# A stack of four graph layers on one core: four batches in one sequence, score rows by way of DRAM, a pace for each stage

## The chip, the cores and the metric

The kernel runs on one core of a Trainium2 chip. The metric is the time of one execution in device microseconds (us). The kernel before was timed three times: 3205.61 us is the median, 3198.1 and 3207.4 the ends. A further execution was taken by the hardware profiler.

The engines by the names of the profile: PE is TensorE (PEld its weight loads), DVE VectorE, ACT ScalarE, POOL GpSimd, SP SyncE, which here only issues transfers. Each engine works through its own queue in order. Work on one waits for another through semaphores.

## The reference

Sixteen batches of 1024 nodes with 256 features (`x`), and one adjacency matrix `adj` (1024 x 1024, a few entries in each row). Four layers, one after the other, all in float32:

```python
# layer 0, h = x: an edge score for each pair of nodes
hidden = relu(h @ W1[:d] per u  +  h @ W1[d:] per v  +  b1)
S   = sigmoid(hidden @ W2 + b2)
a   = einsum('buv,bud->bvd', S * adj, h)
m   = einsum('uv,bud->bvd', adj, h) * h
z   = beta1*h + beta2*(a @ Wa + ba) + beta3*(m @ Wm + bm)
# layer 1
z   = z + relu(einsum('ij,bjd->bid', adj, z) @ W.T + b)
# layers 2 and 3, each with its own weights
f   = z @ W1.T
f1  = f @ W2 + b2
c   = softmax(leaky_relu(f1[:, :, None] + f1[:, None, :]) + adj)
z   = c @ f + bias2 + z
```

Scores are needed only where `adj` is not zero.

## The kernel before

**Groups.** The sixteen batches are four groups of four (`GB`). The time falls into a first stage, and then one pass for each group, which has an edge stage and the layers 1 to 3.

**The scores.** `score_steps` is a generator that computes the edge scores of all groups, one step for one neighbour (a "slot") of 128 nodes in four batches at once. There are 616 steps: 8 that find the neighbours, then 152 for each group. A step is: an indirect gather of 128 rows into a tile `z` by POOL (L695; issued four steps ahead, six tiles), an addition and a product on VectorE (L805, L807), four sums along rows on ScalarE (L811). After the last slot of a tile the sigmoid follows and the results `gt` are put on the list `waiting`, from which indirect scatters write them into a dense matrix `dense_d` in DRAM (L700), one or two behind each gather. At the last tile of a group (L830 to L834) all that still waits is scattered at once, and the group is put on `finished`.

**Pace.** The class `Side` runs these steps along a main stage. Main stages are generators too; each `yield` tells some us of TensorE work, and the steps that are owed are these us times a rate: `RATE[0]`, 0.26, in the first stage and `RATE[1]`, 0.255, in all others. As each engine's instructions stand in the order that this makes (a scheduler of the framework then moves some a little ahead or back by what it holds to be ready), the rate sets how much score work stands between two instructions of a main stage. A group may be used only when its scores are `finished`; where the pace was too low, the missing steps are run with no main stage beside them.

**First stage** (to about 961 us): products that need no scores, for all sixteen batches, with the scores of group 0 and part of those of group 1.

**Edge stage** (`with_edges`): for four column blocks and eight row tiles, `gd` is loaded from `dense_d` by SP (L886), reordered by ScalarE into `gc` (L1064), and multiplied with `hw` into eight banks of PSUM; it waits for all scatters of the group.

**Layers** (`pair_layers`): of a group's four batches two go through layers 1 to 3 and then the other two. For a pair: layer 1 (`projected`, `neighbours`, with `adjT_in` read by SP, L1124), then for layers 2 and 3 and each batch a `front` (features `f` for all nodes, with the node's score as column 257) and two halves of `sums`. In `sums`, VectorE makes a tile `m` from the row `r` of all scores, `ta`, and exp(adj) (L1036, four buffers), TensorE multiplies it with `f` into four banks; then the result is scaled and turned back. `scales` stands between `front` and `sums`: it brings the column of 1024 scores to a row on all partitions by nine 128 x 128 transposes of a broadcast column (L1002, and L1007 for the maximum), and takes the exponentials.

`scales` and `turn_back` are put on the list `later` and are run in the middle of the next stage, by `catch_up` at the second tile of a front or the first of a half. After the fronts of the second pair `ahead` loads `hw` and `z` of the next group (L892, L900), all eight at once on SP.

**Last group.** There are no scores left to compute then. While its first pair goes through the layers, the neighbours' sums of the second pair for six of eight node tiles are computed from lists by gathers and VectorE (`by_lists`, L1172 to L1176, with the first product of a list on ScalarE, L1174), paced by `far_ahead`: 0.88 steps a us for the first 68 us, then 0.58.

Of the kernel before, what the change touches and what calls it, by code (L numbers as in the profile page):

```python
# [19 lines left out]
RATE = (0.26, 0.255)  # L20
# [45 lines left out]
def gnn_stack_kernel(  # L66
# [120 lines left out]
    class Attention:  # L187


        def __init__(self, W1, W2, b2, bias2, name):  # L190
# [5 lines left out]
            self.rows = const.tile([P, DH, P], F32, name=f"{name}_rows")  # L196

        def prepare(self, nat):
# [8 lines left out]
            nc.vector.tensor_copy(self.wT[:, :, D], ps[:, :DH])  # L207
            for dh in range(DH):
                nc.vector.tensor_copy(self.rows[:, dh, :], self.wT[:, dh, D : D + 1].to_broadcast([P, P]))
# [26 lines left out]
    def prepare(t):  # L236
        transpose_weight(l1wT, t[:, 0])
        for i, gat in enumerate((gat2, gat3)):
            gat.prepare(t[:, 1 + i])
# [22 lines left out]
    part_d = dram.tile([XT * P + P, 2 * D], F32, name="part_d")  # L262

# [411 lines left out]
    with tc.If(listed > 0) as arm:  # L675
        with ExitStack() as stack:
# [27 lines left out]
            def score_steps(pool):  # L704
# [75 lines left out]

                moved, got, arrive = None, None, 0
                later = mybir.DependencyClass.NoSync
                for n, (g, t, k) in enumerate(todo):
                    if n + LEAD < len(todo):
                        last = fetch(us, zt, *todo[n + LEAD])
                    for _ in range(0 if n < HOLD else 2 if n % 2 and len(waiting) > 4 else 1):
                        if waiting:
# [3 lines left out]
                            after(tc, ins, [last], later, "behind the gather")  # L791
                    if moving:
# [25 lines left out]
                    if k == slots - 1:  # L818
# [11 lines left out]
                        if t == last_of[g]:  # L830
                            for group, *what in waiting:
                                group.add(scatter(*what))
                            waiting.clear()
                            finished.append(g)  # L834
# [25 lines left out]

            class Side:
# [5 lines left out]
                def along(self, main, rate=1):  # L867
                    for us in main:
                        self.owed += us * rate
# [37 lines left out]
            with ExitStack() as first:  # L907
# [48 lines left out]
                side.along(with_zeros(score_free()), RATE[0])  # L956
# [12 lines left out]
            def front(x, weights):  # L969
# [3 lines left out]
                for jt in range(NT):  # L973
# [7 lines left out]
                    if jt == 1:  # L981
                        catch_up()
                    yield 0.86
                made = {}
                later.append(lambda: scales(f, weights, made))
                return made

            def scales(f, weights, made):
# [4 lines left out]
                ta = small.tile([P, NT], F32, tag="tau", name="tau")  # L993
# [16 lines left out]
                for v in range(NV):  # L1010
                    nc.scalar.activation(r[:, v * HN : (v + 1) * HN], banks[v], AF.Relu, bias=sh[:, 3:4])
                nc.vector.tensor_scalar(sh[:, 1:2], sh[:, 0:1], -0.01, None, ALU.mult)
# [8 lines left out]
            later = []  # L1021

            def catch_up():
                while later:
                    later.pop(0)()

            def sums(made, v, finish):

                if "f" not in made:
                    catch_up()  # L1030
# [3 lines left out]
                for jt in range(NT):  # L1034
# [9 lines left out]
                    if jt == 0:  # L1044
                        catch_up()
# [73 lines left out]
            def neighbours(y, z, cols):  # L1119
                n = cols.stop - cols.start  # L1120
                acc = [[bank() for _ in range(DH)] for _ in range(2)]
                for jt in range(NT):
                    a = three.tile([P, HN], F32, tag="a", name="adjT_in")[:, :n]
                    nc.sync.dma_start(a, adjT_d[jt][:, cols])  # L1124
                    for i in range(2):
                        for eh in range(DH):
# [3 lines left out]
                            )  # L1130
# [315 lines left out]
```

## Time and profile before

| | |
|---|---|
| median of three executions | 3205.61 us |
| the profiled execution, its own time | 3224.95 us |
| its span (first to last instruction) | 3223.1 us |
| granted TensorE clock, mean | 0.990 |
| TensorE busy | 3127.4 us |
| VectorE, ScalarE, POOL busy | 2349.9, 1955.7, 1819.4 us |
| bytes moved | 687.48 MB |

Some groups of the profile, by line:

| line, engine, what | count | busy us | mean ns |
|---|---|---|---|
| L126 PE, products with `m` | 4096 | 923.3 | 383 |
| L126 PE, products with `gc` | 2048 | 456.6 | 384 |
| L1002 PE, transposes in `scales` | 256 | 35.4 | 274 |
| L805 DVE, score, addition | 608 | 738.9 | 1220 |
| L807 DVE, score, product | 608 | 738.0 | 1220 |
| L1036 DVE, `m` | 512 | 375.6 | 744 |
| L811 ACT, score, sums | 2432 | 979.8 | 407 |
| L1064 ACT, `gc` | 128 | 265.2 | 2074 |
| L695 POOL, gathers for scores | 512 | 645.9 | 1261 |
| L700 POOL, scatters | 512 | 642.5 | 1255 |

A float32 product is two instructions in the profile (4096 for 2048 products of the sums), a transpose is one. Matmuls are pipelined, so the mean of one is longer than what it adds: 64 instructions of the sums follow one another in 13.88 us. The edge stages begin at about 961, 1540, 2116 and 2687 us of the span, and the layers follow each.

### The profile page before, as it was taken

To read this page: it belongs to the slowest core of one execution; us is meant where nothing else is said; L and a number is where in the kernel's file an instruction comes from. 1 tells how busy PE (TensorE), PEld (TensorE's weight loads), DVE (VectorE), ACT (ScalarE), POOL (GpSimd) and SP (SyncE) were. 2 spreads that over 40 slices of the span, in tenths; PEclk is the share of its full clock that TensorE was granted. 3 is DMA by queue.
4 is the path that set the end of the run, shared out by engine and by line. 5 is a ranking of instruction groups with operands and counts; after the bars stand their busy time and mean duration, and the time that the engine had idled before them with its cause. 6 is when DMAs were issued, how large, how long until landed. Compare 5 with 4: busy or idle time off the path is not lost. (4 is left out here: it accounts for less than half of the span.)

```text
span 3223.1 us, 39246 instructions
## 1 busy us (share of the span) xinstructions
PE 3127.4 (97%) x12122; PEld 2203.7 (68%) x12122; DVE 2349.9 (73%) x3162; ACT 1955.7 (61%) x6524; POOL 1819.4 (56%) x1483
## 2 busy tenths in 40 slices
PE   8899999999999999999999999899999999998999
PEld 5444544545557668678876867777587688857888
DVE  7797767677774789789768978877798891147744
ACT  3245555666668767567977756688676774413342
POOL 1146778676764656657666665556676652076500
PEclk9999999999999999999999999999999999999999
DMA  9899898888889755756876575587657644485600
GB/s 315 292 323 322 267 288 263 265 242 249 271 284 343 211 167 150 229 158 203 300 233 171 158 212 177 161 284 239 187 151 212 181 145 145 131 256 154 156 7 28
DMA packets 281994, 687.48 MB, mean 213 GB/s; under 512 B 45280, under 2 KB 137440, under 8 KB 274608
## 3 DMA queue, kind: packets, MB, share of 16 engines
q0 software_dynamic: 128224, 387.80, 41.6%
q1 hardware_dynamic: 126112, 245.98, 22.2%
q10 hardware_dynamic: 27440, 51.13, 4.2%
q8 instruction: 97, 1.59, 0.2%
q14 instruction: 121, 0.99, 0.1%
HBM read 553.45 MB, written 131.32 MB: 212 GB/s over the span
## 5 line engine op out<-in xcount | busy, mean ns | idle before, releaser
L811 ACT ACTIVATE z<-z 128x256 f32<-128x256 f32 x2432 | 979.8, 407 | 642.3 <-DVE z L807 568.8
L805 DVE TENSOR_TENSOR z<-z,u 128x1024 f32<-128x1024 f32 x608 | 738.9, 1220 | 435.9 <-PE bank L126 291.9
L126 PE MATMUL bank<-feats,m 128*128 128x257 f32 x4096 | 923.3, 383 | 19.0 <-DVE m L1036 17.8
L695 POOL DMA_INDIRECT z<-v_d,slot_v x512 | 645.9, 1261 | 477.1 <-ACT z L811 264.1
L126 PEld LDWEIGHTS bank<-feats,m 128*128 128x128 f32 x4096 | 771.4, 191 | 138.4 <-DVE m L1036 19.8
L700 POOL DMA_INDIRECT dense_d<-gt,slot_at x512 | 642.5, 1255 | 186.8 <-issue 139.5
L807 DVE SCALAR_TENSOR_TENSOR z<-z,w2r 128x1024 f32<-128x1024 f32 x608 | 738.0, 1220 | 9.0
L126 PE MATMUL bank<-gc,hw 128*128 128x256 f32 x2048 | 456.6, 384 | 25.0 <-ACT gc L1064 17.8
L811 ACT ACTIVATION_READ_ACCUMULATOR z<-z 128x1 f32 x2432 | 463.3, 190 | 0.0
L126 PEld LDWEIGHTS bank<-gc,hw 128*128 128x128 f32 x2048 | 388.6, 192 | 92.5 <-ACT gc L1064 25.9
L126 PE MATMUL bank<-adj_sb,h 128*128 128x512 f32 x1024 | 443.0, 592 | 4.0 <-ACT st L322 2.4
L1036 DVE SCALAR_TENSOR_TENSOR m<-rho,tau,adj_sb 128x512 f32<-128x512 f32 x512 | 375.6, 744 | 72.1 <-PE bank L126 68.5
L126 PE MATMUL bank<-adjT_in,y 128*128 128x512 f32 (+1 forms) x960 | 401.2, 578 | 3.9 <-DMA adjT_in<-adjT_d 2.5
L126 PEld LDWEIGHTS bank<-adj_sb,h 128*128 128x128 f32 x1024 | 194.3, 190 | 244.2 <-issue 239.6
L126 PE MATMUL bank<-w,hT 128*128 128x512 f32 (+1 forms) x1024 | 336.2, 489 | 0.0
L126 PEld LDWEIGHTS bank<-adjT_in,y 128*128 128x128 f32 x960 | 181.9, 190 | 218.9 <-issue 204.3
L1064 ACT ACTIVATE gc<-gd 128x1024 f32<-128x1024 f32 x128 | 265.2, 2074 | 94.0 <-PE bank L126 59.1
L126 PEld LDWEIGHTS bank<-w,hT 128*128 128x128 f32 x1024 | 195.7, 192 | 143.0 <-issue 121.0
L126 PE MATMUL bank<-g_wT,z 128*128 128x257 f32 x1024 | 233.7, 383 | 8.2 <-DVE z L1117 8.2
L695 POOL DMA_INDIRECT z<-v_d,x_node x96 | 123.4, 1285 | 176.7 <-ACT z L811 115.7
L126 PEld LDWEIGHTS bank<-g_wT,z 128*128 128x128 f32 x1024 | 193.2, 191 | 39.0 <-DVE z L1117 8.9
L322 ACT ACTIVATE st<-bank 128x512 f32<-128x512 f32 x128 | 75.6, 590 | 104.3 <-PE bank L126 62.5
(161 smaller groups left out, 2403.2 us busy)
## 6 DMA issues: line engine op xcount, KB each, us to landing
gd<-dense_d SPq DMA_DIRECT2D x128, 512.0 KB
dense_d<-zero ACTq DMA_DIRECT2D x64, 512.0 KB
adjT_in<-adjT_d SPq DMA_DIRECT2D x112, 256.0 KB
h<-in_x_dram SPq DMA_DIRECT2D x19, 1024.0 KB
u_d<-st SPq DMA_DIRECT2D x64, 256.0 KB
v_d<-st SPq DMA_DIRECT2D x64, 256.0 KB
hw_d<-st SPq DMA_DIRECT2D x64, 256.0 KB
u<-u_d POOLq DMA_DIRECT2D x32, 512.0 KB
```

The source lines that it names most:

```text
L126: recent.append(nc.tensor.matmul(*args, **kw))
L322: nc.scalar.activation(st[:, c, :2, :], ps.rearrange("p (s k) -> p s k", s=2), AF.Copy)
L695: return nc.gpsimd.indirect_dma_start(out=dst, out_offset=None, in_=src[:], in_offset=bass.IndirectOffsetOnAxis(ap=at, axis=0), **how,)
L700: return nc.gpsimd.indirect_dma_start(out=dst[:], out_offset=bass.IndirectOffsetOnAxis(ap=at, axis=0), in_=src, in_offset=None,)
L805: paced(nc.vector.tensor_tensor(z, z, u, ALU.add))
L807: nc.vector.scalar_tensor_tensor(zk, zk, 0.0, w2r[:, None, :].to_broadcast([P, GB, D]), ALU.max, ALU.mult)
L811: nc.scalar.activation(zk[:, c, :], zk[:, c, :], AF.Copy, accum_out=s[:, k, c : c + 1])
L1036: nc.vector.scalar_tensor_tensor(m, r[:, cols], ta[:, jt : jt + 1], ea[:, jt, cols], ALU.max, ALU.mult)
L1064: paced(nc.scalar.activation(gc, gd.rearrange("p n i -> p i n"), AF.Copy), 16)
```

## The change

- **Order.** `group_layers` takes the four batches of groups 0 to 2 as one sequence: layer 1 for the first two, the first front, layer 1 for the other two, and then for the eight pairs of layer and batch the next one's front ahead of this one's two halves of sums. `hw` and `z` of the next group are loaded one after the other during the last two of these eight. The last group keeps `pair_layers`.
- **Rows through DRAM.** In `group_layers`, `scales` is replaced by `to_row` (the column and its maximum by one transpose to 9 rows, stored to `row_d`, and read back as a broadcast to all partitions, all on SP) and `from_row`, three ticks later. A tick is every second tile of a half, every fourth of a front, every tile of `neighbours`. The tiles `rows` are then needed only in the other branch of the program, which does not run.
- **Pace.** The rate is chosen by stage: 0.295 in edges and layer 1, 0.26 in fronts, 0.212 in sums. Over a group the steps are about as many as before (136.7 for 136.9).
- **Leftover scatters.** At a group's last tile the waiting scatters are no longer issued at once; they go on behind the following gathers, and the group is `finished` when the last one is out. For the last group they are still issued at once.
- **Lists.** The first product of a list is made by VectorE, and the pace is 0.8 and 0.61.

```diff
-RATE = (0.26, 0.255)
+PACE = dict(free=0.26, edges=0.295, one=0.295, fronts=0.26, sums=0.212)
...
+    row_d = dram.tile([2, B, (NT + 1) * P], F32, name="row_d")
...
                         if t == last_of[g]:
-                            for group, *what in waiting:
+                            ending.append(g)
+                            while waiting and g == NGR - 1:
+                                group, *what = waiting.pop(0)
                                 group.add(scatter(*what))
-                            waiting.clear()
-                            finished.append(g)
+                                done(group)
...
+            def tick():
+                for what in later:
+                    what[0] -= 1
+                while later and later[0][0] <= 0:
+                    later.pop(0)[1]()
...
-                    if jt == 1:
-                        catch_up()
+                    if jt % 4 == 1:
+                        tick()
...
+            def to_row(f, weights, made, row):
+                r = two.tile([P, N], F32, tag="rho", name="rho")
+                tops = two.tile([P, P], F32, tag="tops", name="tops")
+                column = small.tile([P, NT + 1], F32, tag="column", name="column")
+                nc.vector.tensor_copy(column[:, :NT], f[:, :, D])
+                nc.vector.tensor_reduce(column[:, NT:], f[:, :, D], AX.X, ALU.max)
+                ps = bank()
+                nc.tensor.transpose(ps[: NT + 1, :P], column, ident)
+                nc.scalar.activation(r[: NT + 1, :P], ps[: NT + 1, :P], AF.Copy)
+                nc.sync.dma_start(row.rearrange("(t p) -> t p", p=P), r[: NT + 1, :P])
+                nc.sync.dma_start(r, bcast_rows(row[:N], N))
+                nc.sync.dma_start(tops, bcast_rows(row[N:], P))
+                later.append([3, lambda: from_row(f, weights, made, r, tops)])
+
+            def from_row(f, weights, made, r, tops):
+                sh = small.tile([P, 4], F32, tag="shift", name="shift")
+                nc.vector.tensor_reduce(sh[:, 0:1], tops, AX.X, ALU.max)
+                nc.vector.scalar_tensor_tensor(sh[:, 3:4], weights.b2, 2.0, sh[:, 0:1], ALU.mult, ALU.add)
+                nc.scalar.activation(r, r, AF.Relu, bias=sh[:, 3:4])
+                scaled(f, made, r, sh)
...
-                    if jt == 0:
-                        catch_up()
+                    if jt % 2 == 0:
+                        tick()
...
+                    tick()
                     yield 3.4 * n / HN
...
-                        paced(nc.scalar.activation(to, z, AF.Copy, scale=lists(t)[3][:, k : k + 1]))
+                        paced(nc.vector.tensor_scalar(to, z, lists(t)[3][:, k : k + 1], None, ALU.mult))
...
+            def group_layers(g, z):
+                made = {}
+                def fronts(layer, i):
+                    gat = (gat2, gat3)[layer]
+                    steps = front(z[i], gat, row_d[layer, g * GB + i])
+                    made[layer, i] = yield from at_pace("fronts", steps)
+                def both_halves(layer, i):
+                    for v in range(NV):
+                        finish = third(z, i, g * GB) if layer else second(z, i)
+                        yield from at_pace("sums", sums(made[layer, i], v, finish))
+                yield from at_pace("one", layer_one(z[:2]))
+                yield from fronts(0, 0)
+                yield from at_pace("one", layer_one(z[2:]))
+                order = [(layer, i) for layer in range(2) for i in range(GB)]
+                for n, it in enumerate(order):
+                    if n + 1 < len(order):
+                        yield from fronts(*order[n + 1])
+                    if n == 2 * GB - 2:
+                        hw = [load_hw((g + 1) * GB + i) for i in range(GB - 1)]
+                        nz = load_z(g + 1)
+                    if n == 2 * GB - 1:
+                        hw.append(load_hw((g + 1) * GB + GB - 1))
+                        loaded.append((hw, nz))
+                    for _ in range((0, 2, 1)[max(0, n - 2 * GB + 3)]):
+                        load, i = z_loads.pop(0)
+                        load(i)
+                    yield from both_halves(*it)
...
-                        yield us * (0.88 if gone < 68 else 0.58)
+                        yield us * (0.8 if gone < 68 else 0.61)
...
-                side.along(with_edges(g, hw, z), RATE[1])
-                one = pair_layers(g * GB, z[:2], lambda: None, layer_one(z[:2]))
+                side.along(at_pace("edges", with_edges(g, hw, z)))
                 if g < NGR - 1:
-                    side.along(one, RATE[1])
-                    side.along(pair_layers(g * GB + 2, z[2:], lambda: ahead(g + 1), layer_one(z[2:])), RATE[1])
+                    side.along(group_layers(g, z))
```

## The prediction

> **What bounds the kernel now.** I read the page's busy shares, then TensorE's idle time by releaser, then the two largest stalls in order of time, then three stretches of the layers, edge and sum stages, and last the tail.
>
> From the page, busy time by engine, TensorE by slice of the span, and one group of instructions (busy us, mean ns, idle before):
>
> ```profile
> PE 3127.4 (97%) x12122; PEld 2203.7 (68%) x12122; DVE 2349.9 (73%) x3162; ACT 1955.7 (61%) x6524; POOL 1819.4 (56%) x1483
> ...
> PE   8899999999999999999999999899999999998999
> ```
>
> TensorE is the bound: 96 us of 3223.1 are idle. So there are three ways to be faster: less TensorE work, fewer of these 96 us, or less clock lost after a stall. Who TensorE waited for (us in total, times, longest):
>
> ```profile
> PE bank L126 <- DVE m L1036: 17.8, 9, 8.2
> PE bank L126 <- ACT gc L1064: 17.8, 11, 4.9
> ...
> PE bank L126 <- DVE z L1117: 8.2, 2, 8.0
> ```
>
> The largest of each kind, in order of time: end of group 1's layers, then the tail.
>
> ```profile
> 2042.14 0.97 POOL L700 DMA_INDIRECT dense_d<-gt,slot_at  x1 [0.30 <-issue]
> 2043.42 0.97 POOL L695 DMA_INDIRECT z<-v_d,slot_v  x1 [0.30 <-issue]
> ...
> 2048.03 1.23 DVE L805 TENSOR_TENSOR z<-z,u 128x1024 f32<-128x1024 f32 x1 [8.32 <-DMA z<-v_d,slot_v]
> ...
> 2052.43 9.74 PE L126 MATMUL bank<-feats,m 128*128 128x257 f32 x32 [8.19 <-DVE m L1036]
> ```
>
> A run of scatters (L700) fills POOL, the next gather (L695) starts only after it, VectorE stands 8.32 us in order at a score that wants that gather, the `m` behind it is late, and TensorE stands 8.19 us. Clock in the 5 us slices after it: 0.50 and 0.74. Columns below: slice, its us, busy us (and instructions) of PE, PEld, DVE, ACT, POOL, clock, DMA share, GB/s. First two slices of sums, then two of edges:
>
> ```profile
> 1250.00:1275.00 25.00, 25.00 (x125) 21.70 (x124) 24.04 (x39) 18.14 (x66) 20.52 (x16) 1.00 0.55 149
> 1275.00:1300.00 25.00, 24.93 (x124) 21.62 (x123) 24.28 (x36) 17.26 (x69) 20.43 (x16) 1.00 0.73 196
> 1575.00:1600.00 25.00, 25.00 (x117) 22.00 (x117) 17.44 (x18) 24.33 (x60) 12.72 (x12) 1.00 0.85 283
> 1600.00:1625.00 25.00, 25.00 (x117) 21.53 (x116) 18.12 (x23) 24.97 (x58) 11.00 (x10) 1.00 0.85 286
> ```
>
> Beside a full TensorE, VectorE is nearly full in the sums and ScalarE in the edges. So the pace of the scores is a choice between two second bounds.
>
> **Part 1, transposes.** `scales` issues 9 one-pass transposes, `to_row` one. The chain has
>
> ```profile
> 2314.06 0.87 PE bank L1002 x8
> ```
>
> so 8 cost 0.87 us on the path. Groups 0 to 2 have 24 fronts: 24 x 0.87 = **-20.8 us**. The ninth stays as the 9-row transpose. The last group keeps `scales`. On VectorE a copy of 8 columns is added a front, on ScalarE one 0.67 us Relu goes (one of 1.05 us replaces two) and a copy comes: nothing, beside a TensorE that is full. The four copies into `rows` leave the first stage, where VectorE has room.
>
> **Part 2, leftover scatters.** The burst of group 2 cost 8.19 us idle and 2.57 x 0.50 + 5.0 x 0.26 = 2.6 us of clock (busy times of the two slices); that of group 1, at 1412 us, 3.12 us idle and 1.0 us of clock in the same way. The scatters now go one or two behind each gather, and are drained some 10 steps later; by the rates the group is then still some 20 steps ahead of its use. **-14.9 us.** Group 0's burst lies in the first stage (0.6 us idle), group 3's stays.
>
> **Part 3, pace and order in the layers.** I bounded the layer stages by the last edge product of a group and the first of the next: 454.5, 459.7, 446.1 us. Idle TensorE there: 7.5 + 12.3 + 3.3 = 23.1 us. Less the bursts' 11.3, some 11.8 are left, mostly `m` waits at the first sums of a pair (2.03 us at 1172, 2.36 at 1865, 1.13 at 2346), with 2.9 us of clock. A group has 236.8 units of sums; at 0.212 instead of 0.255 these carry 10.2 scores less, each two VectorE instructions of 1.2 us: 24.5 us less VectorE work, its share falls from 0.96 to about 0.86. Fronts now stand one batch ahead of their sums. Of the 14.7 us I take 9: **-9 us** (0 to -15).
>
> **Part 4, pace in the edges.** 108.8 units at 0.295 instead of 0.255 are 4.35 scores more a group. A score occupies ScalarE 4 x 0.40 us, with its share of the `u` copy (1.04 us a tile) 1.72: 7.5 us a group. ScalarE had 107.7 of 114.2 us in group 1's edge stage and 104.7 of 113.0 in most of group 2's, so little of it is free: at most 3 x 7.5 = +22.5. Against it: `gd` loads no longer stand on SP behind the loads of the last two batches, of which TensorE saw 3 us in group 1 and some 7 in group 2. Bounds -9 and +22.5; ScalarE's full slices are the nearer row, but part of the 7.5 falls into its idle: **+6 us**. In `layer_one` the scores at 0.295 take 3.4 us each, POOL 2.5 us for gather and scatter: free.
>
> **Part 5, entry of the last group, and the tail.** TensorE waited 4.87 us at 2687, with 2.3 us of clock, for `gd` behind 16 scatters that began at 2655 when a late `gt` came from VectorE. That burst is not moved, but VectorE should be less late: **-4** (0 to -7). In the tail:
>
> ```profile
> 2909.11 0.72 ACT L1174 ACTIVATE msg<-z,slot_a 128x512 f32<-128x512 f32 x1 [25.11 <-remote]
> ...
> 2912.90 2.51 PE L126 MATMUL bank<-g_wT,z 128*128 128x257 f32 x5 [7.96 <-DVE z L1117]
> ```
>
> ScalarE held the first product of a list until 2909 and with it its own Relu of `r` and VectorE behind both: 7.96 us idle, 2.45 of clock. The product moves to VectorE (0.75 us a piece, 12 of them), and 0.8 for 0.88 thins the list there by 5 steps. What "remote" is the trace does not say; a late gather would hold VectorE just so. **-8** (0 to -10.4).
>
> **Part 6, the row's trip (new wait).** On VectorE's new order stand, behind the column copy and four `m`: the maximum over `tops`, a score, three small operations, then the last two `m` of the half. So VectorE waits for transpose, ScalarE copy, store to DRAM, SP's second issue and a 512 KB broadcast read. I count 0.6 us for the copy, 0.6 for two issues (0.32 each), 2 for a 4.5 KB store (the last stores of the kernel, 512 KB, are issued at 3217.3 and have moved by 3220) and 3.4 for the read (a 512 KB gather whose instruction ended at 1407.3 was used at 1410.7): 6.6 us. After it 0.28 + 0.23 + 0.14 + 0.14 and often a score come ahead of `m`: 2 us. TensorE needs that `m` five products of 1.74 us after the transpose, or 7.4 us where it stands later in the order: 8 on average. 8.6 against 8.0 is 0.6 to 0.7 us at 18 fronts: **+12**. Bounds: none, if the store and read take what shorter waits show (1.96 us for an `adjT_in`), and with the 7.56 us that another `adjT_in` took, 4.8 us a front, +86.
> ScalarE's Relu of `r` waits for the same read; behind it in order stand scores and the evacuation of the half's sums, which TensorE fills only 12 us after the transpose: covered as long as the read is in by then.
> SP's queue is part of it: 72 issues of 0.32 us are nothing to an engine that mostly waits, but order matters. Three fronts (one a group, ahead of the third batch's last sums) follow a `z` load and three `hw` loads, 4 MB, issued about 10 us before the row's store. In the before, such loads moved at 313 to 382 GB/s of which part is gathers:
>
> ```profile
> 2085.00:2090.00 5.00, 5.00 (x26) 4.36 (x25) 5.00 (x11) 4.20 (x17) 1.46 (x2) 1.00 0.90 313
> 2090.00:2095.00 5.00, 5.00 (x25) 4.37 (x24) 5.00 (x9) 2.50 (x10) 3.00 (x3) 1.00 1.00 382
> ```
>
> At 250 for these loads they take 16 us, so the store would stand 6 us longer: 0 to 9 us of stall, I take 5: **+15**. In `neighbours` four `adjT_in` loads stand ahead of the row on SP, so nothing there.
> The Trainium skill, "DMA: Bandwidth & Descriptors", section "Anatomy of one DMA", gives about 2.0 us fixed plus bytes over 436 GB/s; for store and read that estimate is 5.2 us, hidden, and the sum would be 12 us lower. Its section "Queues, rings and completion order" says that descriptors of one ring are consumed in ring order; by that the three stalls are real, and my 15 would be 27. No row of before shows either for a small store.
>
> **Sum:** -20.8 - 14.9 - 9 + 6 - 4 - 8 + 12 + 15 = -23.7 us on an execution of 3224.95 us (span 3223.1): 3201.3. The median shown is 3205.61, 19.3 us below that execution; I put the same difference on it: **3182 us**. For this kernel about 0.3%, 9.6 us, is what a measurement can tell.
>
> **Rivals.**
> *The trip is hidden everywhere* (parts 1 to 5 alone): -50.7, 3155 us. For it: VectorE gets slack in the sums; against: the scheduled order puts `tops` ahead of two `m`.
> *Slower: the trip is long.* Place: VectorE's wait for `tops`. If store and read take 10 us together instead of 5.4, 18 fronts stall 5.2 us instead of 0.65, +82, and the sum is +58: 3264 us; already at 1.3 us more than I count a front the gain of 23.7 is gone. For it: 7.5 us loads in the trace; against: these stand in stages with DMA share 0.75 to 0.9, the sums have 0.45 to 0.7.
> *Edges bound by ScalarE*: +22.5 instead of +6: -7.2, 3198 us, same. For it: 24.97 of 25; against: loads come earlier.
> *The bursts stay* (the leftovers collide with gathers in another way): -8.8, 3197.
>
> **How the numbers follow.** Forecast 0.45 (3160 to 3195), hidden 0.24, long trip 0.18, edges 0.09, bursts 0.04. Faster: 0.44 + 0.24 + a little of the last two 0.01 = 0.69. Same: 0.01 + 0.01 + 0.09 = 0.11. Slower: 0.17 + 0.03 = 0.20. Range: down to the hidden trip with most of the better ends of parts 3 to 5, -70, 3136; up to half of the long trip, +28, 3234.
>
> **What would show it.** 24 transposes of 9 rows and 64 instead of 256 of L1002's kind. No wait of 3 us or more for `m` behind a run of scatters. VectorE about 86% in sums, ScalarE full in edges. Idle VectorE before the maximum over `tops`: up to 5 us harmless, TensorE's `m` waits right after it are the price. The prediction is wrong if these sum to over 50 us, or if edge stages grow over 120 us.

## The result, and the profile after

The changed kernel takes 3240.41 us (median of six executions, 3232.5 to 3245.12) against 3205.76 us for the kernel before (six, 3198.1 to 3210.26): the ratio is 1.0108, its 95% interval 1.0091 to 1.0125. It is 34.6 us slower; the forecast was 23.7 us faster.

From the page of the changed kernel, its busy times (span 3243.4 us, mean granted clock 0.987, before 0.990):

```profile
PE 3119.7 (96%) x11930; PEld 2187.8 (67%) x11930; DVE 2366.1 (73%) x3194; ACT 1946.2 (60%) x6512; POOL 1832.2 (56%) x1483
```

TensorE has fewer instructions and less busy time, but 123.7 us of idle instead of 95.7. Who it waited for (us in total, times, longest):

```profile
PE bank L128 <- ACT st L1303: 29.7, 16, 6.6
PE bank L128 <- ACT gc L1122: 21.3, 19, 3.5
PE bank L1273 <- ACT val L1266: 18.5, 17, 3.4
...
PE bank L128 <- DVE m L1094: 5.9, 7, 1.6
```

The waits for `m` (17.8 us before) are nearly gone. New are `st` and `val`, the evacuations of finished sums (ScalarE copies them out of PSUM, scaled by `share`), 48.2 us together against 5.5 before:

```profile
PE bank L126 <- ACT st L1249: 3.1, 5, 1.5
...
PE bank L1219 <- ACT val L1212: 2.4, 4, 0.9
```

A typical one in the changed kernel, in order of time, from stretches of the layers of group 1 (start, us, engine, line, what; in brackets the idle time before it and what ended it):

```profile
1844.00 0.43 SPq L1039 DMA_DIRECT2D tops<-row_d  x1
...
1851.23 0.29 DVE L1044 TENSOR_REDUCE shift<-tops 128x1 f32<-128x128 f32 x1 [4.88 <-DMA tops<-row_d]
...
1851.75 1.22 DVE L820 TENSOR_TENSOR z<-z,u 128x1024 f32<-128x1024 f32 x1
...
1851.79 1.15 ACT L1046 ACTIVATE rho<-rho,shift 128x1024 f32<-128x1024 f32 x1 [5.10 <-DVE shift L1045]
...
1854.31 3.30 ACT L1082 ACTIVATE feats<-feats 128x256 f32<-128x256 f32 x8
...
1854.68 0.16 DVE L1107 RECIPROCAL share<-bank 128x1 f32<-128x1 f32 x1
...
1859.12 0.46 ACT L1266 ACTIVATE val<-bank,share 128x256 f32<-128x256 f32 x1
...
1859.63 0.33 PE L1273 MATMUL bank<-ident,val 128*128 128x128 f32 x1 [3.39 <-ACT val L1266]
```

Read it from the bottom. TensorE stands 3.39 us for `val`. `val` needs the reciprocal `share` (L1107) from VectorE and a turn on ScalarE. VectorE stood 4.88 us at the maximum over `tops`, because the read that SP issued at 1844.00 was in only by 1851.2. The reciprocals are behind that maximum in VectorE's order, with a score and an `m` between. ScalarE stood 5.10 us for the same shift, and then had its whole block on the row (Relu, Exp, eight scalings, 5.8 us) and a score's sums ahead of `val`. So one late read holds two engines, and the evacuation needs both. Here the first `share` was there at 1854.84, and ScalarE's order came last.

Where 4 MB of loads stand ahead of the store, the same happens with larger numbers (end of group 0's layers):

```profile
1477.08 1.44 SPq L916 DMA_DIRECT2D hw<-hw_d  x3
...
1487.97 0.29 SPq L1037 DMA_DIRECT2D row_d<-rho  x1
...
1496.96 0.32 SPq L1038 DMA_DIRECT2D rho<-row_d  x1
...
1502.47 0.28 DVE L1044 TENSOR_REDUCE shift<-tops 128x1 f32<-128x128 f32 x1 [7.53 <-DMA tops<-row_d]
...
1504.13 0.16 DVE L1107 RECIPROCAL share<-bank 128x1 f32<-128x1 f32 x1
...
1505.94 6.43 PE L128 MATMUL bank<-feats,m 128*128 128x257 f32 x15 [6.57 <-ACT st L1303]
```

A `z` load of 1 MB went out just ahead of the three of `hw`. The store of 4.5 KB takes 9.0 us to the issue that waits for it; the two others behind such loads took 8.4 and 6.1 us, and the 21 with no such loads ahead 1.3 to 5.2 us, 2.8 in the median.

VectorE had 89% of two slices in the sums (forecast 86%) and ScalarE was full beside the edges (two slices each; columns as before):

```profile
1240.00:1265.00 25.00, 23.10 (x109) 19.34 (x107) 22.19 (x35) 15.43 (x54) 17.58 (x12) 1.00 0.62 174
1265.00:1290.00 25.00, 25.00 (x123) 21.85 (x122) 22.44 (x34) 17.02 (x71) 11.30 (x9) 1.00 0.48 127
1580.00:1605.00 25.00, 23.93 (x107) 19.50 (x107) 19.07 (x22) 23.89 (x64) 20.12 (x17) 1.00 0.90 290
1605.00:1630.00 25.00, 25.00 (x113) 20.48 (x112) 20.14 (x22) 25.00 (x64) 15.54 (x10) 1.00 0.87 298
```

By stage, in each profiled execution: an edge stage runs from the first to the last product of `gc` of a group, its layers from there to the next group's first.

| us | before | after |
|---|---|---|
| edges, groups 0, 1, 2 | 125.9, 116.0, 120.2 | 130.4, 126.5, 124.6 |
| layers, groups 0, 1, 2 | 453.2, 459.9, 451.3 | 465.8, 464.6, 451.0 |
| last group | 535.8 | 523.7 |

### The profile page after: what moved, and what is told of

Read it like the earlier page. It is cut to its first block, busy times and chain, and to the rows that moved or that the text cites. A ratio compares the mean times of both kernels' runs of the same rounds, so it can differ in the third digit from the quotient of the medians.

```text
span 3243.4 us, 38951 instructions
## 1 busy us (share of the span) xinstructions
PE 3119.7 (96%) x11930; PEld 2187.8 (67%) x11930; DVE 2366.1 (73%) x3194; ACT 1946.2 (60%) x6512; POOL 1832.2 (56%) x1483
## 4 chain that ended last, share of the span: by engine, by line
PE 69%; ACT 10%; DMA 10%; DVE 8%; issue 2%; SPq 0%; POOL 0%; ACTq 0%; DVEq 0%; POOLq 0%
PE bank L128 66%; ACT z L826 4%; DMA tops<-row_d 3%; DVE z L820 2%; DMA gd<-dense_d 2%; ACT feats L1082 2%; DMA row_d<-rho 2%; ACT gc L1122 1%; DVE z L822 1%; DMA adjT_in<-adjT_d 1%; DVE slot_a L448 1%; PE bank L1273 1%; DVE m L1094 1%; DVE left L450 1%; ACT rho L1046 1%
## 5 line engine op out<-in xcount | busy, mean ns | idle before, releaser
L703 POOL DMA_INDIRECT z<-v_d,slot_v x512 | 627.1, 1225 | 528.9 <-ACT z L826 280.3
L822 DVE SCALAR_TENSOR_TENSOR z<-z,w2r 128x1024 f32<-128x1024 f32 x608 | 738.1, 1221 | 9.9
L128 PE MATMUL bank<-gc,hw 128*128 128x256 f32 x2048 | 468.0, 390 | 31.6 <-ACT gc L1122 21.3
L128 PEld LDWEIGHTS bank<-gc,hw 128*128 128x128 f32 x2048 | 390.3, 194 | 108.7 <-ACT gc L1122 42.4
L703 POOL DMA_INDIRECT z<-v_d,x_node x96 | 132.8, 1384 | 136.9 <-ACT z L826 77.3
L708 POOL DMA_INDIRECT dense_d<-gt,x_at x96 | 124.9, 1301 | 29.3 <-issue 25.9
```

What stands on the lines that cost most here:

```text
L128: recent.append(nc.tensor.matmul(*args, **kw))
L703: return nc.gpsimd.indirect_dma_start(out=dst, out_offset=None, in_=src[:], in_offset=bass.IndirectOffsetOnAxis(ap=at, axis=0), **how,)
L708: return nc.gpsimd.indirect_dma_start(out=dst[:], out_offset=bass.IndirectOffsetOnAxis(ap=at, axis=0), in_=src, in_offset=None,)
L822: nc.vector.scalar_tensor_tensor(zk, zk, 0.0, w2r[:, None, :].to_broadcast([P, GB, D]), ALU.max, ALU.mult)
```

## The experiments

Ratios are to the kernel before, run on the same chip in the same comparison (its median was 3204.5 to 3223.1 us from chip to chip, so times of different comparisons are set against each other by these ratios; 0.001 is 3.2 us). Edges and layers are the sums over groups 0 to 2 in the one profiled execution and are not corrected for the chip, which can make up to 0.6% of them, 8 us in the layers; `st`+`val` is what TensorE waited for these two together. "ScalarE's block pinned" and "both pinned" are orders set by hand, told below.

| kernel | edges | layers | `st`+`val` | ratio, interval |
|---|---|---|---|---|
| before | 362.1 | 1364.4 | 5.5 | 1 |
| after | 381.5 | 1381.4 | 48.2 | 1.0108, 1.0091 to 1.0125 |
| row undone | 380.2 | 1326.9 | 5.6 | 0.9930, 0.9906 to 0.9954 |
| pace undone | 360.9 | 1378.0 | 16.3 | 1.0031, 1.0018 to 1.0045 |
| six steps to the row's use | 380.1 | 1344.2 | 25.6 | 0.9977, 0.9956 to 0.9998 |
| before + leftovers + lists | 362.7 | 1339.6 | 4.9 | 0.9913, 0.9897 to 0.9930 |
| row and pace undone | 367.4 | 1347.0 | 10.9 | 0.9923, 0.9897 to 0.9948 |
| before + leftovers | 364.8 | 1344.3 | 3.3 | 0.9945, 0.9927 to 0.9963 |
| 4 MB behind the row | 381.4 | 1369.6 | 42.4 | 1.0044, 1.0027 to 1.0061 |
| 4 MB behind, six steps | 379.9 | 1338.8 | 25.7 | 0.9934, 0.9911 to 0.9958 |
| 4 MB behind, ScalarE's block pinned | 383.1 | 1340.4 | 20.2 | 0.9928, 0.9901 to 0.9955 |
| the same, milder pace | 372.8 | 1353.2 | 25.4 | 0.9922, 0.9893 to 0.9951 |
| row undone, `scales` late | 380.8 | 1347.7 | 19.0 | 1.0063, 1.0042 to 1.0083 |
| row undone, edges slow | 356.2 | 1347.0 | 12.8 | 0.9906, 0.9879 to 0.9934 |
| 4 MB behind, both pinned | 378.7 | 1312.1 | 5.0 | 0.9888, 0.9870 to 0.9905 |
| both pinned, 4 MB ahead | 381.6 | 1318.2 | 7.8 | 0.9914, 0.9898 to 0.9931 |
| both pinned, edges slow | 352.4 | 1343.1 | 8.7 | 0.9908, 0.9891 to 0.9925 |
| `tops` behind `share`, four steps | 380.8 | 1315.2 | 7.8 | 0.9889, 0.9860 to 0.9919 |
| both pinned, edges 0.265 | 362.9 | 1321.8 | 4.1 | 0.9872, 0.9841 to 0.9904 |

**Undoing one part.** The row undone:

```diff
-                    steps = front(z[i], gat, row_d[layer, g * GB + i])
+                    steps = front(z[i], gat)
```

> The changed kernel with the nine transposes of `scales` in place of the row's trip through DRAM; all else is kept. Theory (the trip): in the changed kernel VectorE waits 56 us for `tops` at 21 fronts, ScalarE stands in order at its Relu of `r` for the same thing, the evacuations behind it (`st`, `val`) come late, and TensorE waits 48 us for these, with some 10 us of clock. Without the trip these waits fall to the 6 us of the kernel before, and the transposes cost 20.8 us again: 3240 - 52 + 21, about 3209 us. Rival (the order): it is the sequence of four batches, with a front ahead of each two halves, that puts evacuations late; then the waits for `st` and `val` stay and the time rises by the transposes to about 3261 us.

Measured 0.9930, so the theory of the trip holds, and the gain is larger than the 31 us expected: the row costs 0.0178, 57 us, though it takes transposes off TensorE. Nearly all of that is in the layers (54.5 us).

The pace undone:

```diff
-PACE = dict(free=0.26, edges=0.295, one=0.295, fronts=0.26, sums=0.212)
+PACE = dict(free=0.26, edges=0.255, one=0.255, fronts=0.255, sums=0.255)
```

> The changed kernel with one pace of 0.255 in all stages after the first. Theory: the three edge stages were 5.0, 10.7 and 4.5 us longer than before because ScalarE is full there; they come back to 125.7, 116.2 and 120.5 us and the kernel to about 3220 us, while the waits for `st` and `val` stay near 48 us. Rival (the fuller sums): with 10 scores a group more in the sums VectorE and ScalarE are late there and the trip hides less, so the sums lose what the edges win or more: 3240 to 3260 us.

Measured 1.0031, so the pace costs 25 us in the changed kernel. The edges give back 20.6; in the layers `st` and `val` do not stay near 48 us but fall to 16.3, and `m` rises to 28.6 (20 times). VectorE's wait at `tops` falls from 56.1 to 40.3 us.

More steps between the read and its use (and due entries of `later` run whatever stands ahead of them):

```diff
-                later.append([3, lambda: from_row(f, weights, made, r, tops)])
+                later.append([6, lambda: from_row(f, weights, made, r, tops)])
```

> The changed kernel with six ticks in place of three between `to_row` and `from_row`, and a list that lets other entries pass one that is not due. The same work; only the consumers of the trip stand later. Theory (the trip): VectorE's wait for `tops` falls from 56 us to under 15, TensorE's waits for `st` and `val` from 48 to under 20, and the time to about 3200 us. Rival (the order): TensorE's waits for `st` and `val` stay and the time stays at 3235 to 3245 us.

Measured 0.9977, 42 us better than the changed kernel: the distance matters. But VectorE still stands 33.7 us at `tops`, and 25.6 us of `st` and `val` remain, the longest 7.6; both were forecast lower.

The leftover scatters (`finished` is then filled when a group's last one is issued) and the lists of the tail, put on the kernel before:

```diff
-                            for group, *what in waiting:
-                                group.add(scatter(*what))
-                            waiting.clear()
-                            finished.append(g)
+                            ending.append(g)
...
-                        paced(nc.scalar.activation(to, z, AF.Copy, scale=lists(t)[3][:, k : k + 1]))
+                        paced(nc.vector.tensor_scalar(to, z, lists(t)[3][:, k : k + 1], None, ALU.mult))
...
-                        yield us * (0.88 if gone < 68 else 0.58)
+                        yield us * (0.8 if gone < 68 else 0.61)
```

> The kernel before with two parts of the change alone: leftover scatters behind gathers, and the lists' first product on VectorE with the paces 0.8 and 0.61. By the prediction's parts 2 and 5 (14.9 and 8 us) about 3183 us; by the tail that the changed kernel shows (12 us shorter from the last group's edges on) 3179. Rival: the leftover scatters only move the wait, and the gain is that of the lists alone, 3195 us or above.

Measured 0.9913, 28 us. Then the first hunk of it alone, and the changed kernel with both of the first two diffs, row and pace undone:

> The kernel before with the leftover scatters put behind gathers and nothing else. Theory: 3206 - 15 = 3191 us, and the longest wait for `m`, 8.2 us, is gone; the other 10 us of the run with both (3182) are the lists of the tail. Rival: the scatters give all of it (3182) and the lists nothing, or the lists most of it (3200 or more).

> The changed kernel with its row undone and its pace undone: the order of four, the leftover scatters and the lists of the tail are left. Theory: the pace costs the edge stages and gives the layers nothing, so the edges come back to about 117 to 127 us (from 123 to 135 with the row alone undone) and the layers stay at 440 to 445: about 3187 - 17 = 3170 us; against the kernel with the old order (3182) the order is then worth some 11. Rival: the slower sums of the changed kernel need their pace, as the waits for `m` (28.6 us) showed with the row still in: then 3185 or more, and waits for `m` of over 20 us.

The scatters alone give 0.9945 (18 us, no wait for `m` over 2.4 us), so the lists give some 10. With the order of four it is 0.9923: the order itself gives nothing that can be told (0.0010, within both intervals), and 3170 was wrong. Beside the row undone (0.9930) the pace is neutral when no row is there: 13 us more in the edges, 20 less in the layers (some 6 of these are the chip's: it runs the kernel before 0.5% slower).

**The 4 MB.** The `hw` and `z` loads of the next group are made by `load_ahead`, one step after the last row, and ordered behind its reads; the second of these runs has the six steps from above as well:

```diff
-                    if n == 2 * GB - 2:
-                        hw = [load_hw((g + 1) * GB + i) for i in range(GB - 1)]
-                        nz = load_z(g + 1)
+                    if n == 2 * GB - 2:
+                        later.append([2, load_ahead])
```

> The changed kernel with the 4 MB of `hw` and `z` of the next group issued behind the last row's reads of each group instead of ahead of its store. Theory (queue): the store of these three rows lands in about 2 us instead of 9, the stalls of 6.6, 2.4 and 3.6 us go, with the clock lost behind them about 16 us: 3224. Rival (ScalarE's order in every front): the three are part of a loss spread over 21 fronts, and 3237 or more remains.

> The changed kernel with six steps instead of three between the row's reads and their use, and the 4 MB behind the last row's reads. Theory: with six steps alone 3199 us, longest wait behind ScalarE's evacuation 7.6 us: that is the queue's part, and it goes: 3188. Waits of TensorE for `st` and `val` together under 10 us. Rival: the longest wait has another cause and 3199 remains.

Measured 1.0044 (0.0064 or 20.5 us better; the three stores take 1.5, 2.6 and 2.1 us instead of 9.0, 8.4 and 6.1, and the longest wait for `st` falls from 6.6 to 3.5) and, with six steps as well, 0.9934. Both times are what the queue theory said (3224 and 3188 expected; 1.0044 and 0.9934 of 3206 are 3220 and 3185). But `st` and `val`, forecast under 10 us with six steps, stayed at 25.7, and the second run is only where the kernel without a row stands: the transposes saved still don't show.

**Whose order.** Three runs ask whether the place of ScalarE's block is the price. In the first, with the 4 MB behind and four steps, it is put behind the evacuations of the half that is ending (`last_out`), and so are the two Exp that read the shift; a second run gives that a milder pace. In the third the old transposes are back and only `scales` is made late, with no trip at all:

```diff
-                nc.scalar.activation(r, r, AF.Relu, bias=sh[:, 3:4])
+                ins = nc.scalar.activation(r, r, AF.Relu, bias=sh[:, 3:4])
+                after(tc, ins, last_out, mybir.DependencyClass.NoSync, "behind the copies")
...
+PACE = dict(free=0.26, edges=0.265, one=0.27, fronts=0.26, sums=0.24)
...
-                    later.append([1, lambda: scales(f, weights, made)])
+                    later.append([4, lambda: scales(f, weights, made)])
```

> The changed kernel with the 4 MB behind the last row's reads, four steps between the reads and their use, and ScalarE's whole block on the row (Relu, the three Exp, the scalings) put behind the four evacuations of the half that is ending. Theory: the row cost its time by where ScalarE's block stood, before the evacuations; behind them, waits of TensorE for `st` and `val` fall under 8 us together (from 25.7 with the 4 MB moved and six steps), and the 20.8 us of transposes that the row saves show for the first time: the run without the row stood at 0.993 of the kernel before, so 0.993 - 0.0065 = 0.9865. Rival: the row's use of the DMA queues or of DRAM costs it, wherever ScalarE reads it: 0.993 as with six steps.

> The same with the pace between the old and the new: edges 0.265, first products 0.27, fronts 0.26, sums 0.24. Theory: the pace of 0.295 costs the edges 14 to 20 us over three groups and 0.212 gives the layers up to 21; in between, edges at about 121 us each, layers at 436 to 440: 0.985 or a little less. Rival: `m` waits come back as with 0.255 everywhere (28.6 us): 0.990.

> The changed kernel with its row undone (0.993 of the kernel before) and the old block of transposes, Relu, Exp and scalings made four steps later than it was, so that it stands before the evacuations at the end of the half, with no trip through DRAM and no read to wait for. Theory, if the block's place alone is the price: waits of TensorE for `st` and `val` of 20 us or more (5.6 with the row undone), 1.000. Rival, if it is the wait for the read that ScalarE stands in: the block takes 6 us and is through in time, 0.993 and waits under 8 us.

The first pinned run stays at 0.9928 with 20.2 us of waits: the theory that ScalarE's place alone is the price fell (0.9865 and under 8 us were expected). What the pin itself is worth is not shown: the run is 0.0116 better than the one with the 4 MB behind and three steps, but it has a fourth step too. The rival, that the DMAs cost it wherever the row is read, falls with the next runs. The milder pace moves time from edges to layers and no more (0.985 was expected). The late `scales` cost 0.0133, 43 us, of which at most 21 are in the layers; 27 are in the last group (551 us against 524), where `scales` serves sums that come at once (both on a chip 0.5% slower than that of the row undone). It shows that this block made late is dear without any DMA, not how dear the row's was.

What still held TensorE in the pinned run, in order of time (same columns):

```profile
1826.06 0.29 DVE L1052 TENSOR_REDUCE shift<-tops 128x1 f32<-128x128 f32 x1 [3.96 <-DMA tops<-row_d]
...
1828.37 1.22 DVE L822 SCALAR_TENSOR_TENSOR z<-z,w2r 128x1024 f32<-128x1024 f32 x1
1829.51 0.16 DVE L1118 RECIPROCAL share<-bank 128x1 f32<-128x1 f32 x1
...
1829.68 0.42 ACT L826 ACTIVATE z<-z 128x256 f32<-128x256 f32 x1 [7.26 <-DVE share L1118]
...
1831.30 0.45 ACT L1278 ACTIVATE val<-bank,share 128x256 f32<-128x256 f32 x1
...
1831.80 1.93 PE L1286 MATMUL bank<-ident,val 128*128 128x128 f32 x6 [3.56 <-ACT val L1278]
...
1832.96 1.15 ACT L1054 ACTIVATE rho<-rho,shift 128x1024 f32<-128x1024 f32 x1
```

Here ScalarE's Relu comes after `val`, and yet `val` is late: ScalarE itself stood 7.26 us at a score's first sum, four of which it has ahead of `val`. The view names the reciprocal as the releaser, but the sum needs that score's product (L822), which ended at 1829.59. Both came late because VectorE had stood at `tops`. So the maximum was put behind the reciprocals of the half that is ending, and with that also behind the score and the `m` among them. The first run below adds this to the pinned one ("both pinned"), the second is the same with the 4 MB where the changed kernel has them, the third is the changed kernel with this edit and four steps, and nothing pinned on ScalarE:

```diff
+                    last_share[:] = [nc.vector.reciprocal(share[:, c : c + 1], acc[c][:, D : D + 1])]
...
+                ins = nc.vector.tensor_reduce(sh[:, 0:1], tops, AX.X, ALU.max)
+                after(tc, ins, last_share, mybir.DependencyClass.NoSync, "behind the shares")
```

> The run with the 4 MB behind the reads, four steps, and ScalarE's block behind the evacuations, and now also VectorE's maximum over `tops` put behind the four reciprocals (`share`) of the half that is ending. Theory: what remained there (waits of TensorE for `st` and `val` of 20.2 us, 0.9928) was VectorE standing at `tops` with the reciprocals behind it, so that the evacuations waited for their scale; those waits fall under 8 us and 0.9928 goes to about 0.988. Rival: ScalarE is simply too full at the end of a half (scores and evacuations), the reciprocals don't matter: 0.992 or more and over 15 us of such waits.

> The changed kernel with four steps and both places pinned (maximum over `tops` behind the reciprocals, ScalarE's block behind the evacuations), and the 4 MB left ahead of the row's store. Theory: with the reciprocals ahead of it a row that is 9 us late in one front of eight still holds VectorE and the `m` behind it, but two or three of these stalls only, some 6 to 10 us over the run with the 4 MB moved: 0.990 to 0.991. Rival: the 4 MB cost what they cost in the changed kernel, 20 us: 0.994.

> The changed kernel with one thing moved: VectorE's maximum over `tops` comes behind the four reciprocals of the half that is ending (and four steps behind the reads instead of three, so that it can). The 4 MB stay ahead, nothing is pinned on ScalarE, the pace is the changed kernel's. Theory: this order on VectorE is the whole of the loss beside the 4 MB, so it gives what both pins gave with the 4 MB ahead, 0.9914; waits for `st` and `val` under 10 us. Rival: ScalarE's own place has a part in it: 0.995 or more.

Measured 0.9888, 0.9914 and 0.9889. The last, with one order changed and one step more, is 70 us faster than the changed kernel, on ratios. Six steps without the order gave 42, so 28 us are beyond what distance gave; four steps without it were not run. `st` and `val` are 7.8 us together, and VectorE stands 14.2 us at `tops`. A place of the same kind in its trace:

```profile
1822.84 0.42 SPq L1041 DMA_DIRECT2D tops<-row_d  x1
...
1828.60 0.16 DVE L1110 RECIPROCAL share<-bank 128x1 f32<-128x1 f32 x1
...
1830.67 0.27 DVE L1046 TENSOR_REDUCE shift<-tops 128x1 f32<-128x128 f32 x1
...
1830.99 1.18 ACT L1269 ACTIVATE val<-bank,share 128x256 f32<-128x256 f32 x3
...
1831.10 1.20 PE L1276 MATMUL bank<-ident,val 128*128 128x128 f32 x6
...
1833.00 1.15 ACT L1049 ACTIVATE rho<-rho,shift 128x1024 f32<-128x1024 f32 x1
```

The read has 7.8 us and nobody waits for it at this place; the Relu follows the shift, so ScalarE's block falls behind the evacuations without being pinned. The 4 MB cost nothing here that can be told (0.9889 against 0.9888), or 8 us (0.9914): the two runs with them ahead differ by no more than their intervals allow. The store was still late in this trace (issued 1473.61, read issued 1483.51), but TensorE lost 2.32 us behind it, by `m`, not 6.57.

Now the transposes show. The first of three stretches of layers and the sum of the three, for the row undone and then for both pinned with the 4 MB behind (columns as before; the pace is the same):

```profile
1091.70:1534.60 442.90, 439.88 (x1866) 335.87 (x1865) 380.85 (x514) 303.31 (x1120) 272.37 (x215) 1.00 0.61 182
...
sum 1326.90, PE 1319.56 PEld 1008.15 DVE 1130.89 ACT 899.10 POOL 841.06; mean PE 439.85 PEld 336.05 DVE 376.96 ACT 299.70 POOL 280.35
```

```profile
1081.00:1518.30 437.30, 432.93 (x1802) 328.71 (x1801) 378.21 (x520) 301.81 (x1118) 274.22 (x214) 1.00 0.65 196
...
sum 1312.10, PE 1299.08 PEld 986.70 DVE 1125.79 ACT 899.02 POOL 840.02; mean PE 433.02 PEld 328.90 DVE 375.26 ACT 299.68 POOL 280.01
```

64 products and 6.8 us of TensorE fewer in each group, 20.5 us in three. Of these the stages get 14.8 us shorter.

**Pace again.** Turned the other way (edges 0.22, first products, fronts and sums 0.264), without the row and then with both places pinned; and last a small step, the second line:

```diff
+PACE = dict(free=0.26, edges=0.22, one=0.264, fronts=0.264, sums=0.264)
+PACE = dict(free=0.26, edges=0.265, one=0.295, fronts=0.26, sums=0.222)
```

> The changed kernel with its row undone and the pace turned the other way: edges 0.22 instead of 0.295, first products, fronts and sums 0.264. Theory: the edges are bound by ScalarE's copies behind the scores, 0.295 against 0.255 cost them 14 us without the row and 20 with it, so 0.22 gives back another 12 over three groups, about 116 us each; the layers have the slack in ScalarE and VectorE for 0.009 more: 0.9885 of the kernel before. Rival: the layers take it back in waits for `m`, `st` and `val`, as 0.255 lost 20 us there against 0.212: 0.9925 or more, layers at 450 or above.

> The run with both places pinned and the 4 MB behind the reads, with the pace of the run without the row that turned it the other way (edges 0.22, the rest 0.264; 0.9906). Theory: the two gains add, edges about 118 us and layers 441 to 445: 0.985. Rival: at 0.264 the layers with the row run into waits for `m`, as the run with the pace undone did (28.6 us): 0.991 or more.

> Both places pinned and the 4 MB behind the reads, as the run at 0.9888, with the edges' pace alone lowered from 0.295 to 0.265 and the sums' raised from 0.212 to 0.222. Theory: 0.03 less in the edges gives 3 us a group, 0.01 more in the sums costs under 1 us of waits for `m` there: 0.9865. Rival: the layers have no slack for it, as at 0.264 (35 us): 0.990 or more.

0.9906, 0.9908 and 0.9872, where 0.9885, 0.985 and 0.9865 were expected. Each of the first two is set against the same kernel at 0.295 and 0.212: without the row the edges give 24 us and the layers take 20 back; with it the edges give 26 and the layers take 31 (`m` 12.2 us; the 35 of the last expectation is a misreading), so the two gains do not add. The small step gives 16 in the edges and loses 10 in the layers, which one wait of 11.4 us for `gc` at the end of group 2 accounts for. It is the fastest version here, 3164.35 us on a chip where the kernel before takes 3207.09; it can't be told from the run at 0.9888, and its interval still meets those of the best two with no row (0.9906 and 0.9913).

## Why the prediction was wrong

**Parts 2 to 5** summed to -29.9; with only the row undone they gave -22 (-30 to -15). Leftover scatters: -14.9 forecast, -18 alone. Last group, the 4 and 8 us of part 5: 12.1 us shorter (535.8 to 523.7), and the lists alone some 10. Pace in the edges: +6 was mis-sized. The edges grew by 19.4: the pace alone costs 20.6, near its bound of 22.5, as ScalarE's full slices said, and with the pace undone the edges are 1.2 us shorter than before (360.9 for 362.1), where the earlier loads had a bound of 9. Pace and order in the layers: -9 forecast, 12.7 less than with the kernel before's pace and order (1339.6 to 1326.9) where no row stands, and for the pace alone a loss of 3.4 where it does (1378.0 to 1381.4).

**Part 1** was right in size: 20.5 us of TensorE for 20.8 (24 x 0.87 is 20.9). It was hidden by part 6.

**Part 6** is the step that failed: +27 for the row's trip, and with part 1 +6.2; measured +57. That is 51 of the 58 us between forecast and result. It followed VectorE's wait at `tops` to TensorE by `m` alone and put the path by the evacuations at nothing.

- The list of what stands behind `tops` on VectorE was "a score, three small operations, then the last two `m`". It left out the reciprocals, and with them the evacuations, and it did not follow that score to ScalarE, where its sums stand ahead of an evacuation. VectorE's waits there (56.1 us, 21 times) were seen coming; that they reach TensorE as `m` was the error: 5.9 us by `m`, 48.2 by `st` and `val`.
- "covered as long as the read is in by then", of ScalarE's Relu, was the sentence that excused it. The read was not in by then, and the block behind the Relu is 5.8 us long, which was not counted.
- The trip was counted at 6.6 us. Its store took 2.8 us in the median where no loads were ahead (2 were counted) and its read 4.5 (up to 7.2; 3.4 were counted) from issue to landing, with the copy and the issues some 8.5. By the prediction's own path these 1.9 us more, at 18 fronts, are another 34 us of waits for `m`, of which the trace has 5.9 in all.
- The three fronts behind 4 MB were forecast at 15 us; moving the loads gave 20.5, with its mechanism (the stores above). With the reciprocals ahead, the same late stores cost 0 to 8.

The signs that were to show it followed the same path: waits for `m` over 50 us, of which 5.9 came. The other sign, an edge stage over 120 us, came in all three groups (130.4, 126.5, 124.6), though two of them stood at 120 or more before.

The Trainium skill, "DMA: Bandwidth & Descriptors", "Anatomy of one DMA", gave an estimate of 5.2 us for store and read; measured are 7.3. The page fits its figures to transfers issued from GpSimd, and these are issued from SP. By the prediction's own reckoning 5.2 us in place of 5.4 would also have taken some 4 us off the sum and not 12. Its section "Queues, rings and completion order", by which descriptors of one ring are consumed in ring order, agrees with the 9.0 us.

The rival that the trip is hidden everywhere stood at 3155; with VectorE's order mended the kernel comes to 0.9888 or 0.9889, about 3170. The rival of the long trip had the right sign, and the 1.3 us more a front at which it let the gain go were passed by the 1.9 measured, but its stall was put on `m` at VectorE: that the time came out on its side is in part luck.

Open is why the pace costs 25 us beside the row in the changed kernel and 2 without it. The edges take 20.6 of the 25; the layers win some 14 to 20 by it without the row and lose 3.4 with it. With fewer scores in the sums VectorE comes to `tops` earlier and stands there longer (56.1 us, and 40.3 with the pace undone); that fits, but no run separates it. The shares of the two engines are not settled either. With ScalarE's block pinned, VectorE's order took the waits for `st` and `val` from 20.2 to 5.0 us, but the ratios (0.9928 and 0.9888) have intervals that just meet. ScalarE's place was never changed by itself beside the row; made late with no row it cost up to 21 us in the layers. Nor does any run part the reciprocals from the score that the same order moves ahead of the maximum.

## What to carry to other kernels

When a wait is put on an engine that works in order, list all that its queue holds behind it, the small operations too: here four reciprocals of 0.16 us, which the evacuations need, and a score, whose sums stand ahead of an evacuation on ScalarE. TensorE waited 48.2 us for evacuations, by way of these and of ScalarE's block on the row, and 5.9 for the large tiles. Then follow each of them to the bound engine. Where such a wait can't be avoided, issue the read early and place its first use just behind the operations that release the bound engine, not at the earliest place where it may be ready: here that order with one step more of distance was worth 70 us, and three steps more without it 42.

## What the runs showed of the hardware

A 4.5 KB store took 1.3 to 5.2 us (median 2.8), and 9.0, 8.4 and 6.1 us (9.9, 10.4 and 6.1 in the run with one order changed) with 4 MB issued some 10 us earlier on the same queue. Some short waits cost clock as well: in the changed kernel one of 2.37 us was followed by a 5 us slice at 0.66 (from 1900.69 on), another of 2.37 us by one at 1.00 (from 1785.80 on). The mean granted clock was 0.987 in the changed kernel and 0.994 with both places pinned; taken as time, an estimate, that is 0.7% of the span or some 22 us, beside 49 us less waiting for `st`, `val` and `m`; the spans differ by 77.1, on two chips. The same kernel before took 3204.5 to 3223.1 us in the median from chip to chip, which is as much as most of the effects told of here.
